# Layer 0 of a four-layer gated cross-attention network: the order of the last row transfers out, and the grain of the adds of the rows that come back

## The chip, the cores and the metric

The kernel runs on one core of a Trainium2 chip. A core has five engines that matter here, each with its own list of instructions that it runs strictly in order: TensorE (PE, matrix products), VectorE (DVE), ScalarE (ACT), GpSimd (POOL) and SyncE (SP), which issues transfers. Transfers run on sixteen DMA engines beside them. The metric is the device time of one execution in microseconds, lower is better; the number given is the median of several executions.

## The reference, cut to what matters

The input x has 16 sequences of 128 tokens and 128 features. Four layers follow one another, each an attention to a context and a feed-forward part, both added to x through a gate:

```python
x = x + tanh(g_xattn[0]) * _L0_xattn_ref(_layernorm(x), ctx)
x = x + tanh(g_ffn[0])   * _L0_ffn_ref(_layernorm(x), Wr, Wg, Wu, Wd)
x = x + tanh(g_xattn[1]) * _L1_xattn_ref(_layernorm(x), ctx, ...)
x = x + tanh(g_ffn[1])   * _L1_ffn_ref(_layernorm(x), ...)
...   # layers 2 and 3: two more attentions, a slot mixture, a second routed feed-forward

# _L0_ffn_ref: 8 experts, each token uses 2 of them
topk_vals, topk_idx = top_k(flat @ Wr, 2);  topk_w = softmax(topk_vals)
combine = sum(one_hot(topk_idx, 8) * topk_w)
out = sum over e of  (silu(flat @ Wg[e]) * (flat @ Wu[e])) @ Wd[e] * combine[:, e]
```

What matters for the change is that the feed-forward part of layer 0 sends each token to two of eight experts, and that its result is added to x before the attention of layer 1 normalizes x. The feed-forward part of layer 1 has 16 routed experts and two shared ones.

## The kernel before, in words

**Groups.** The 16 sequences form four groups of four (512 tokens). X[g] holds a group's x in on-chip memory as 128 partitions x 4 sequences x 128 features. Work on different groups is interleaved: the attention of one group runs while the experts of another fill TensorE.

**Layer 0, feed-forward.** Group 0 is computed densely, all 8 experts (16 half-experts of width 128) for all tokens. Groups 1 to 3 (`BYE` = 1) are computed sparsely: `choose_0` normalizes and routes them, `places_0` counts tokens by expert and gives every (token, choice) a row in a table `xd` in device memory, sorted by expert. Twenty-four indirect transfers on GpSimd (line 941, one for each of 12 sequences and 2 choices) scatter the rows into `xd`. `blocks_0` loads `xd` back in blocks of 128 rows by SP (line 1005), transposes them on TensorE (line 1012), multiplies each with the weights of its one expert (lines 1034 and 989) and writes the result to `yd` (line 997). `return_0` gathers the rows back with 24 indirect transfers on GpSimd (line 1072), and VectorE adds each, times its weight, to X[g] (line 1064).

**Experts.** `experts` is one stream of all dense experts, in the order of `ORDER`. `gated` (lines 445 to 471) does one half-expert n: two matrix products `pg` and `pu` (lines 450, 451), a gating `sg` on ScalarE and VectorE (lines 455 to 458), the product `h` on VectorE (lines 460, 462), and its weighting by the routing `hw`, on GpSimd (line 470), or on VectorE (line 468) for a few experts that `on_vector` names. `hw` is left out for the shared experts, which in layer 1 are n = 0 and 1. The third product `acc` follows `LAG` = 2 experts later (line 1089). The weight of the routing reaches the chip's partitions through a transfer `cb` (line 433). After each expert the stream takes some steps of other work that is listed for that n: routing of the next group, and from three lists the steps of the sparse part. `SEND` says after which experts of group 0 of layer 0 a scatter is issued (15 of 24; the other 9 follow after the last expert, in the loop `for _ in sending`). `FETCH` says after which experts of layer 1 a gather is issued: two each after n = 0 to 3 of group 0, one each after n = 4 to 17, and one each after n = 0 and 1 of group 1. `ADD` says where the adds are written: those of group 1 at n = 6 of group 0, of group 2 at n = 14, of group 3 at n = 4 of the next.

**Main order.** The main program pulls the stream with `until(layer, g)` until that group's result is in X[g], then writes the instructions of the next attention, for example `until(0, 0); attention_1(0); until(0, 1); attention_1(1)`. The stream stops at every `yield what`, so what the attention writes comes between two pieces of it. An attention begins with `normed`: statistics of X[g] on VectorE, `ve` (line 255), the power `rs` on GpSimd (line 257), and the scaling `xn` on VectorE (line 268); `transposed` follows on TensorE (line 241) and `add_row` adds a bias to X[g] on GpSimd (line 279).

**What sets the order.** When the program is built, a planner orders each engine's instructions: it simulates the engines with its own costs, and gives a free engine the ready instruction that was written earliest. An instruction that is written late but ready early can thus be placed ahead of others. The order is fixed on the chip. `behind_of(what, ins)` adds an edge to it: `ins` is placed behind the last instruction recorded in `latest[what]`, on the same engine, without a wait. `latest["h"]` is the last product h, `latest["hw"]` the last hw on GpSimd. Scatters and gathers are ordered behind the hw last written. Of the eight adds of a group only the first (t = 0, k = 0) is ordered behind an h; the second of a sequence follows the first because both write the same part of X[g].

Buffers with one tag share their place. The normalized rows that the scatters read (`xs`, in `choose_0`) have the tag `kTm` with one place, which the keys `kT` of the first attention of layer 1 use next.

Of the kernel before, what the change touches and what calls it, by code (L numbers as in the profile page):

```python
# [14 lines left out]
ALU = mybir.AluOpType  # L15
# [4 lines left out]
GB = 4  # L20
# [14 lines left out]
BYE = 1  # L35
# [24 lines left out]
def flamingo(ctx, tc, x_in, ctx_in, mask_in, w1, w2, w3, wslot, wsmall, slots, cols_in, rows_in, consts_in,  # L60
# [51 lines left out]
    def behind_of(what, ins):  # L112

        if what in latest:
            in_turn([latest[what]], ins)
# [130 lines left out]
    def normed(g, xn=None, on_act=False):  # L246
        x = X[g]
        st = small.tile([P, GB, 6], F32, tag=tag_of("st"), name="st")
        mv = small.tile([P, GB, 2], F32, tag=tag_of("mv"), name="mv")
        for t in range(GB):  # L250
            nc.vector.bn_stats(st[:, t, :], x[:, t, :])  # L251
        for t in range(GB):
            nc.vector.bn_aggr(mv[:, t, :], st[:, t, :])
        ve = small.tile([P, GB], F32, tag=tag_of("ve"), name="ve")
        nc.vector.tensor_scalar(ve[:], mv[:, :, 1], EPS, None, ALU.add)  # L255
        rs = small.tile([P, GB], F32, tag=tag_of("rs"), name="rs")
        nc.gpsimd.tensor_tensor(rs[:], ve[:], neghalf[:], ALU.pow)  # L257
        if xn is None:
            xn = act.tile([P, GB, D], F32, tag=tag_of("xn"), name="xn", bufs=1)
        if on_act:  # L260
            off = small.tile([P, GB], F32, tag="off", name="off")
            nc.gpsimd.tensor_tensor(off[:], mv[:, :, 0], rs[:], ALU.mult)
            nc.gpsimd.tensor_scalar(off[:], off[:], -1.0, None, ALU.mult)
        for t in range(GB):
            if on_act:
                nc.scalar.activation(xn[:, t, :], x[:, t, :], AF.Identity, bias=off[:, t:t + 1], scale=rs[:, t:t + 1])
            else:
                nc.vector.tensor_scalar(xn[:, t, :], x[:, t, :], mv[:, t, 0:1], rs[:, t:t + 1], ALU.subtract, ALU.mult)  # L268
        return xn
# [588 lines left out]


    SEND = [(n, 1 + (n + 1) % 2) for n in range(6, 16)]  # L860
    FETCH = {0: [(n, 2) for n in range(4)] + [(n, 1) for n in range(4, 18)], 1: [(0, 1), (1, 1)]}
    ADD = {0: [(6, 1), (14, 2)], 1: [(4, 3)]}

    def on_vector(layer, g, n):

# [39 lines left out]
    def places_0():  # L905
# [32 lines left out]
        for t in range(NT):  # L938
            for k in range(2):
                yield  # L940
                ins = nc.gpsimd.indirect_dma_start(  # L941
                    out=xd[:], out_offset=bass.IndirectOffsetOnAxis(ap=to[:, k, t:t + 1], axis=0), in_=xs[:, t, :],
                    in_offset=None)
                apart("xd", ins)
                behind_of("hw", ins)

    def owners_0():
        tmp, v, nb, two, comb, to = placed[0]
# [105 lines left out]
    def return_0():  # L1054

        to, by, _ = places[0]
        for g in range(BYE, NG):
            tags = ("ya", "yb") if (g - BYE) % 2 else ("xns", "xnTs")
            ys = [act.tile([P, GB, D], F32, tag=tag, name="y0", bufs=1) for tag in tags]
            t0 = (g - BYE) * GB  # L1060
            def add(g=g, t0=t0, ys=ys):
                for t in range(GB):
                    for k, y in enumerate(ys):
                        ins = nc.vector.scalar_tensor_tensor(X[g][:, t, :], y[:, t, :], by[:, k, t0 + t:t0 + t + 1],
                                                             X[g][:, t, :], ALU.mult, ALU.add)
                        if not t and not k:
                            behind_of("h", ins)
            adds[g] = add

            for t in range(GB):  # L1070
                for k, y in enumerate(ys):
                    ins = nc.gpsimd.indirect_dma_start(
                        out=y[:, t, :], out_offset=None, in_=yd[:],
                        in_offset=bass.IndirectOffsetOnAxis(ap=to[:, k, t0 + t:t0 + t + 1], axis=0))
                    apart(f"y{g}{k}", ins)
                    behind_of("hw", ins)
                    yield

    adds = {}

    def experts():

# [22 lines left out]
        for at, (layer, g) in enumerate(ORDER):  # L1105
# [22 lines left out]
            if layer == 1:  # L1128
                for n, k in FETCH.get(g, ()):
                    steps.setdefault(n, []).extend([("x", fetching, None)] * k)  # L1130
                for n, i in ADD.get(g, ()):
                    steps.setdefault(n, []).append(("x", i, (0, i)))
            acc = []
            for n, (w, k) in enumerate(FW[layer]):
                side[0] = "x"
# [13 lines left out]
                if late and n == LAG:  # L1149
                    late()  # L1150
                for side[0], step, what in steps.get(n, ()):
                    owners_0() if step == "owners" else adds[step]() if isinstance(step, int) else next(step, None)
                    side[0] = "m"
                    if what is not None:
                        yield what
            if moving:
                side[0] = "m"
                for _ in sending:
                    pass
                side[0] = "x"  # L1160
                while behind:
                    down()
                what = end()
                side[0] = "m"
                yield what
                nxt = routing(1, 0)
                for n, _ in enumerate(blocks_0()):
                    if n in (8, 11, 12, 15):
# [243 lines left out]
```

## Time and profile before

| | |
|---|---|
| median of 3 runs | 922.02 us (920.46 to 922.61) |
| profiled execution | 919.22 us, its span 917.5 us |
| granted TensorE clock over the span | 0.972 |
| scatters, line 941 | 24, median 969 ns on GpSimd, landing 2.3 us (median) after issue |
| gathers, line 1072 | 24, median 982 ns on GpSimd, landing 2.4 to 6.7 us after issue, median 3.7 |
| adds of returned rows, line 1064 | 24, median 351 ns, up to 1358 |
| hw on GpSimd, line 470 | 137, mean 1287 ns |

A row of a timeline gives start, length, engine, line, operation, written tile and read tiles, shapes and count, and in brackets how long the engine idled before it and what ended that. A row of waits gives who waited for whom, then the total, the number and the longest wait. A row of the stretch table gives a stretch, its length, the busy time of PE, PE's weight loads, DVE, ACT and POOL with instruction counts, the TensorE clock that was granted as a share of full speed, the busy share of the DMA engines and GB/s. Times count from the span's start. An engine that is not the bottleneck may idle at no cost.

### The profile page before, as it was taken

How to read it: one execution, taken by the hardware profiler on the slowest of the kernel's cores; microseconds unless marked ns; L12 is line 12 of the kernel's file. 1: busy time of each engine (PE TensorE's matmuls, PEld its weight loads, DVE VectorE, ACT ScalarE, POOL GpSimd, SP SyncE). 2: the span in 40 equal slices, each digit the busy share in tenths (PEclk: the TensorE clock that was granted, in tenths of full speed). 3: DMA queues.
4: the chain of work that ended last, by engine and by line, in shares of the span. 5: the costliest groups of instructions: out<-in, count | busy, mean ns of one | idle time of the engine just before them, and what ended most of it. 6: DMA issues, size and time to landing. Idle time of an engine off the chain costs nothing.

```text
span 917.5 us, 16089 instructions
## 1 busy us (share of the span) xinstructions
PE 831.0 (91%) x6191; PEld 464.1 (51%) x6191; DVE 571.5 (62%) x1598; ACT 266.3 (29%) x484; POOL 302.0 (33%) x312
## 2 busy tenths in 40 slices
PE   5897599889879999999999999999989999999997
PEld 4553399335335454455455545555554544454443
DVE  4673244566777647567686777668666668666522
ACT  2522355231313222322223222233212331222321
POOL 5448421456533114112422113231114123313443
PEclk9899699899999999999999999999999999999999
DMA  9351122631211002101202112310102111211231
GB/s 303 125 124 39 54 70 77 214 111 49 70 53 58 25 2 81 36 25 35 73 22 70 40 43 85 101 36 25 36 13 73 48 36 46 83 48 48 95 106 32
DMA packets 55677, 62.12 MB, mean 68 GB/s; under 512 B 14312, under 2 KB 33512, under 8 KB 55472
## 3 DMA queue, kind: packets, MB, share of 16 engines
q1 hardware_dynamic: 53536, 57.67, 20.5%
q0 software_dynamic: 1536, 3.15, 1.1%
q8 instruction: 49, 0.80, 0.4%
q10 hardware_dynamic: 528, 0.26, 0.1%
q14 instruction: 28, 0.23, 0.1%
HBM read 53.97 MB, written 7.09 MB: 67 GB/s over the span
## 4 chain that ended last, share of the span: by engine, by line
PE 48%; DVE 20%; POOL 13%; issue 9%; DMA 5%; ACT 4%; POOLq 0%; SPq 0%; DVEq 0%; ACTq 0%
PE mm L108 8%; POOL hw L470 6%; PE acc L1089 6%; PE pg L450 6%; PE pu L451 5%; DVE mp L490 3%; DVE sg L456 3%; PE mm L617 2%; PE po L496 2%; POOL xd L941 2%; DVE h L462 2%; DMA y<-yd,to 2%; POOL rs L257 2%; PE po L499 2%; PE mm L612 2%
## 5 line engine op out<-in xcount | busy, mean ns | idle before, releaser
L470 POOL TENSOR_TENSOR hw<-h,cb 128x512 f32<-128x512 f32 x137 | 176.2, 1287 | 443.5 <-DVE h L462 353.7
L451 PE MATMUL pu<-xnTx,wall 128*128 128x512 f32 x288 | 154.4, 618 | 10.5 <-DVE sg L456 9.0
L450 PE MATMUL pg<-xnTx,wall 128*128 128x512 f32 x288 | 153.4, 615 | 1.1 <-ACT xnTx L243 0.7
L1089 PE MATMUL acc<-hw,wall 128*128 128x512 f32 x288 | 152.2, 612 | 1.5 <-POOL hw L470 1.5
L455 ACT ACTIVATE sg<-pg 128x512 f32<-128x512 f32 x123 | 73.4, 598 | 240.2 <-PE pg L450 236.4
L462 DVE TENSOR_TENSOR h<-sg,pu 128x512 f32<-128x512 f32 x145 | 99.0, 683 | 54.8 <-PE pu L451 35.6
L456 DVE SCALAR_TENSOR_TENSOR sg<-sg,pg 128x512 f32<-128x512 f32 x123 | 83.5, 679 | 48.7 <-ACT sg L455 48.4
L451 PEld LDWEIGHTS pu<-xnTx,wall 128*128 128x128 f32 x288 | 51.9, 194 | 72.5 <-issue 39.8
L1089 PEld LDWEIGHTS acc<-hw,wall 128*128 128x128 f32 x288 | 54.4, 196 | 60.8 <-issue 52.4
L490 DVE TENSOR_REDUCE mp<-mm 128x4 f32<-128x512 f32 (+1 forms) x112 | 65.8, 644 | 21.1 <-PE mm L617 19.9
L450 PEld LDWEIGHTS pg<-xnTx,wall 128*128 128x128 f32 x288 | 49.7, 192 | 42.4 <-issue 29.8
L504 DVE RECIPROCAL rcw<-po 128x128 f32<-128x128 f32 (+1 forms) x28 | 25.2, 899 | 53.6 <-PE po L499 42.6
L639 ACT ACTIVATE pts<-mm 128x512 f32<-128x512 f32 x64 | 33.8, 602 | 77.1 <-PE mm L633 77.0
L496 PE MATMUL po<-pts,vp 128*32 128x128 f32 (+1 forms) x896 | 46.0, 273 | 7.0 <-ACT pts L639 6.5
L257 POOL TENSOR_TENSOR rs<-ve,neghalf 128x4 f32<-128x4 f32 x32 | 32.9, 1027 | 58.8 <-DVE ve L255 55.0
L268 DVE TENSOR_SCALAR xn<-x,mv,rs 128x128 f32<-128x128 f32 x96 | 33.1, 402 | 24.1 <-POOL rs L257 24.1
L499 PE MATMUL po<-pts,own 128*32 128x128 f32 (+1 forms) x896 | 44.1, 265 | 0.6 <-issue 0.6
L241 PE MATMUL tr<-ident,xn 128*128 128x128 f32 x100 | 22.4, 310 | 19.2 <-DVE xn L268 17.0
L496 PEld LDWEIGHTS po<-pts,vp 128*32 128x32 f32 (+1 forms) x896 | 21.4, 108 | 30.3 <-ACT pts L639 14.8
L251 DVE BATCH_NORM_STATS2 st<-x 128x6 f32<-128x128 f32 x128 | 29.3, 280 | 7.4 <-DMA x<-in_x 6.8
L458 ACT ACTIVATE sg<-pg 128x512 f32<-128x512 f32 x33 | 19.5, 595 | 48.8 <-PE pg L450 48.6
L241 PEld LDWEIGHTS tr<-ident,xn 128*128 128x128 f32 x100 | 12.6, 142 | 35.9 <-issue 14.6
(346 smaller groups left out, 1249.4 us busy)
## 6 DMA issues: line engine op xcount, KB each, us to landing
cb<-combD SPq DMA_DIRECT2D x72, 256.0 KB, 3.3
cb<-combD SPq DMA_DIRECT2D x128, 128.0 KB, 2.9
wall<-in_gu SPq DMA_DIRECT2D x24, 256.0 KB, 4.4
wall<-in_dn SPq DMA_DIRECT2D x12, 256.0 KB, 4.3
xb<-xd SPq DMA_DIRECT2D x7, 256.0 KB, 2.8
yd<-yb SPq DMA_DIRECT2D x7, 256.0 KB, 2.5
xd<-vp SPq DMA_DIRECT2D x1, 1072.0 KB, 7.6
x<-in_x SPq DMA_DIRECT2D x4, 256.0 KB, 4.7
```

The lines of the kernel that those rows point to most:

```text
L108: nc.tensor.matmul(out=o, lhsT=l, rhs=r, start=start, stop=stop)
L257: nc.gpsimd.tensor_tensor(rs[:], ve[:], neghalf[:], ALU.pow)
L450: in_turn(chain, nc.tensor.matmul(out=pg[:], lhsT=w[:, 0], rhs=xnT[:], start=True, stop=True))
L451: in_turn(chain, nc.tensor.matmul(out=pu[:], lhsT=w[:, 1], rhs=xnT[:], start=True, stop=True))
L455: nc.scalar.activation(sg[:], pg[:], AF.Tanh, scale=0.5)
L456: nc.vector.scalar_tensor_tensor(sg[:], sg[:], 1.0, pg[:], ALU.add, ALU.mult)
L462: ins = nc.vector.tensor_tensor(h[:], sg[:], pu[:], ALU.mult)
L470: latest["hw"] = nc.gpsimd.tensor_tensor(hw[:], h[:], cb[:], ALU.mult).ins
L490: nc.vector.tensor_reduce(mp[:, 0:n, 32 * i + 16:32 * i + 18], src, AX.X, ALU.max)
L496: in_turn(chain, nc.tensor.matmul(out=po[32 * jj:32 * jj + 32, 0, :], lhsT=vcols, rhs=pts, start=first, stop=last, skip_group_check=True))
L499: in_turn(chain, nc.tensor.matmul(out=po[32 * jj:32 * jj + 32, 1, :], lhsT=own[rows, r, :], rhs=pts, start=False, stop=last, skip_group_ch ...
L1089: in_turn(chain, nc.tensor.matmul(out=acc[0][:], lhsT=w[:, 2], rhs=h[:], start=n == 0, stop=last))
```

## The change

The scatters: after the last expert of group 0 of layer 0 four instead of nine are written at once. The other five are written after the stream has yielded, which is after the first attention of layer 1 has been written, and are ordered behind `latest["rs"]`, the power of that attention's norm, instead of behind an hw. `normed` records that power.

The adds: instead of eight at a time from `ADD`, each is written on its own. `return_0` keeps a list of gathers written; once it holds more than four, each further gather's step also writes the oldest one's add, ordered behind the h last written. Four more steps write the last four. `FETCH` for group 1 of layer 1 is one step after each of n = 0 to 5, of which the first two write a gather and an add and the other four an add alone. When the last add of a group is written the stream reports the group as done, which is at n = 7 and n = 15 of group 0 and n = 5 of group 1, instead of n = 6, 14 and 4. Numbers of gathers, scatters and adds stay.

```diff
--- before.py
+++ after.py
@@ -254,7 +254,7 @@
         ve = small.tile([P, GB], F32, tag=tag_of("ve"), name="ve")
         nc.vector.tensor_scalar(ve[:], mv[:, :, 1], EPS, None, ALU.add)
         rs = small.tile([P, GB], F32, tag=tag_of("rs"), name="rs")
-        nc.gpsimd.tensor_tensor(rs[:], ve[:], neghalf[:], ALU.pow)
+        latest["rs"] = nc.gpsimd.tensor_tensor(rs[:], ve[:], neghalf[:], ALU.pow).ins
         if xn is None:
             xn = act.tile([P, GB, D], F32, tag=tag_of("xn"), name="xn", bufs=1)
         if on_act:
@@ -858,8 +858,7 @@
 
 
     SEND = [(n, 1 + (n + 1) % 2) for n in range(6, 16)]
-    FETCH = {0: [(n, 2) for n in range(4)] + [(n, 1) for n in range(4, 18)], 1: [(0, 1), (1, 1)]}
-    ADD = {0: [(6, 1), (14, 2)], 1: [(4, 3)]}
+    FETCH = {0: [(n, 2) for n in range(4)] + [(n, 1) for n in range(4, 18)], 1: [(n, 1) for n in range(6)]}
 
     def on_vector(layer, g, n):
 
@@ -942,7 +941,9 @@
                     out=xd[:], out_offset=bass.IndirectOffsetOnAxis(ap=to[:, k, t:t + 1], axis=0), in_=xs[:, t, :],
                     in_offset=None)
                 apart("xd", ins)
-                behind_of("hw", ins)
+                behind_of(sent_behind[0], ins)
+
+    sent_behind = ["hw"]
 
     def owners_0():
         tmp, v, nb, two, comb, to = placed[0]
@@ -1054,29 +1055,31 @@
     def return_0():
 
         to, by, _ = places[0]
+        landed = []
+
+        def add():
+
+            g, t, k, y = landed.pop(0)
+            i = (g - BYE) * GB + t
+            behind_of("h", nc.vector.scalar_tensor_tensor(X[g][:, t, :], y, by[:, k, i:i + 1], X[g][:, t, :], ALU.mult,
+                                                          ALU.add))
+            return g if (t, k) == (GB - 1, 1) else None
+
         for g in range(BYE, NG):
             tags = ("ya", "yb") if (g - BYE) % 2 else ("xns", "xnTs")
             ys = [act.tile([P, GB, D], F32, tag=tag, name="y0", bufs=1) for tag in tags]
-            t0 = (g - BYE) * GB
-            def add(g=g, t0=t0, ys=ys):
-                for t in range(GB):
-                    for k, y in enumerate(ys):
-                        ins = nc.vector.scalar_tensor_tensor(X[g][:, t, :], y[:, t, :], by[:, k, t0 + t:t0 + t + 1],
-                                                             X[g][:, t, :], ALU.mult, ALU.add)
-                        if not t and not k:
-                            behind_of("h", ins)
-            adds[g] = add
-
             for t in range(GB):
                 for k, y in enumerate(ys):
+                    i = (g - BYE) * GB + t
                     ins = nc.gpsimd.indirect_dma_start(
                         out=y[:, t, :], out_offset=None, in_=yd[:],
-                        in_offset=bass.IndirectOffsetOnAxis(ap=to[:, k, t0 + t:t0 + t + 1], axis=0))
+                        in_offset=bass.IndirectOffsetOnAxis(ap=to[:, k, i:i + 1], axis=0))
                     apart(f"y{g}{k}", ins)
                     behind_of("hw", ins)
-                    yield
-
-    adds = {}
+                    landed.append((g, t, k, y[:, t, :]))
+                    yield add() if len(landed) > 4 else None
+        while landed:
+            yield add()
 
     def experts():
 
@@ -1128,8 +1131,6 @@
             if layer == 1:
                 for n, k in FETCH.get(g, ()):
                     steps.setdefault(n, []).extend([("x", fetching, None)] * k)
-                for n, i in ADD.get(g, ()):
-                    steps.setdefault(n, []).append(("x", i, (0, i)))
             acc = []
             for n, (w, k) in enumerate(FW[layer]):
                 side[0] = "x"
@@ -1149,20 +1150,25 @@
                 if late and n == LAG:
                     late()
                 for side[0], step, what in steps.get(n, ()):
-                    owners_0() if step == "owners" else adds[step]() if isinstance(step, int) else next(step, None)
+                    done = owners_0() if step == "owners" else next(step, None)
+                    if step is fetching and done:
+                        what = (0, done)
                     side[0] = "m"
                     if what is not None:
                         yield what
             if moving:
                 side[0] = "m"
-                for _ in sending:
-                    pass
+                for _ in range(4):
+                    next(sending)
                 side[0] = "x"
                 while behind:
                     down()
                 what = end()
                 side[0] = "m"
                 yield what
+                sent_behind[0] = "rs"
+                for _ in sending:
+                    pass
                 nxt = routing(1, 0)
                 for n, _ in enumerate(blocks_0()):
                     if n in (8, 11, 12, 15):
```

## The prediction, made before the changed kernel was run

> **What bounds the kernel now.** I read the page's busy shares first, then the chain of work that ended last, then idle time by engine in each stretch, then the timelines of GpSimd (POOL), VectorE (DVE) and TensorE (PE) around the two edits.
>
> ```profile
> span 917.5 us, 16089 instructions
> PE 831.0 (91%) x6191; PEld 464.1 (51%) x6191; DVE 571.5 (62%) x1598; ACT 266.3 (29%) x484; POOL 302.0 (33%) x312
> ```
>
> TensorE is the bound overall, so time can only come out of stretches where it idles or runs at a reduced clock. The stretch table gives it 1.73 us busy of 14 between 87 and 101 us, 105.1 of 124 between 161 and 285, and 146.8 of 155 between 285 and 440. The edits touch the first two.
>
> First hole, in the order DVE, POOL, PE (start, length, operation, and in brackets the idle time before it):
>
> ```profile
> 91.42 0.21 DVE L255 TENSOR_SCALAR ve<-mv 128x4 f32<-128x4 f32 x1
> ...
> 98.32 0.97 POOL L941 DMA_INDIRECT xd<-xs,to  x1 [0.31 <-issue]
> 99.31 1.06 POOL L257 TENSOR_TENSOR rs<-ve,neghalf 128x4 f32<-128x4 f32 x1
> ...
> 101.17 1.15 PE L241 MATMUL tr<-ident,xn 128*128 128x128 f32 x4 [11.77 <-DVE xn L268]
> ```
>
> The norm's input `ve` is there at 91.63, but its power `rs` starts at 99.31: ten scatters stand ahead of it from 86.82 on, and TensorE idles 11.77 us.
>
> The second stretch, waits between 161 and 285 us (total, times, longest):
>
> ```profile
> DVE x L1064 <- DMA y<-yd,to: 19.8, 10, 3.3
> ...
> PE pu L451 <- DVE sg L456: 7.0, 2, 3.8
> ...
> PE mm L108 <- DVE aT L578: 4.7, 1, 4.7
> ```
>
> VectorE stood 19.8 us ahead of the adds of returned rows, each with its gather still in flight. Behind it TensorE stopped three times: 3.81 us until 174.84, 3.16 until 204.53 and 4.74 until 255.45, and each stop is followed by a stretch at about half clock (column after POOL: PEclk):
>
> ```profile
> 174.50:181.50 7.00, 6.66 (x9) 2.79 (x10) 5.32 (x16) 0.60 (x1) 3.94 (x4) 0.54 0.60 166
> 204.50:208.50 4.00, 3.97 (x9) 1.87 (x10) 2.63 (x5) 0.00 (x0) 2.96 (x3) 0.57 0.06 24
> 255.40:260.10 4.70, 4.65 (x13) 2.79 (x14) 3.62 (x14) 0.64 (x2) 0.78 (x1) 0.64 0.01 2
> ```
>
> Time lost to the clock is length x (1 - clock): 7.0 x 0.46 = 3.2, 4.0 x 0.43 = 1.7, 4.7 x 0.36 = 1.7 us. So the three stops cost 7.0, 4.9 and 6.4 us.
>
> **Why the adds run early.** They are written at experts 6 and 14 of group 0 and expert 4 of group 1, but only the first of each eight is ordered behind an `h`. The other six (t = 1, 2, 3) have no order, and the planner put them where it believed their rows had landed: one group's stand at 173.8 to 178.6, before expert 6.
>
> **Part 1, five scatters move behind `rs`.** A scatter takes 0.97 us and 0.30 to the next, 1.27. Five fewer ahead of `rs` bring it from 99.31 to 99.31 - 6.35 = 92.96, still after `ve` (91.63), so the whole shift counts for the norm. The five left then follow: rs 1.06, scatters 6.35, and probably the bias add L279 (1.27), written earlier and ready once `xn` is done. Last scatter: starts about 100.8 instead of 98.32, lands 2.3 later at 103.1. Who waits: the row loads xb on SP's queue (issued at 100.61 before, landing at least 2.8 us later), so rows are there at 105.9; and the keys kT of this attention, whose buffer is the one the scatters read from (108.33 - 6.35 = 102.0 wanted, 103.1 possible, 1.1 us). TensorE transposed the first rows at 110.06, because attention held it until then; now attention's scores end near 104.8 and the rows come at 105.9. Gain 110.06 - 105.9 = **4.2 us**. Bounds: 6.35 if the scatters' tail is hidden; -2.5 if the planner puts the first row transposes ahead of attention, so that all of it waits for the later scatter. I take 4.2, the value that both timelines give. The clock brings nothing: the hole is still near 5.4 us, longer than all three stops above that ended cold. 101.8 to 105.9 holds attention, so no second hole but 1 us.
>
> **Part 2, each add alone, behind its own `h`, four gathers later.** The 24 adds stay (0.35 us), as do the 24 gathers, their order behind `hw` and their queue; removed is the freedom to run early. Add i now stands behind h of expert i from i = 4 on; gather i behind hw of expert i - 4. An expert takes six matmul halves, 3 x 0.86 = 2.57 us, so four are 10.3 us at least; gathers 8 to 23 landed 3.3 to 5.5 us after issue. So none of these is waited for.
> - Stop 2 (add at 200.22, gather issued 195.50): gone, 4.9 us.
> - Stop 3 (adds at 250.10, 252.53, 254.45, which held the attention's aT at 254.72 while its input was there at 249): they now follow h of experts 3, 4, 5 of group 1. Gone, 6.4 us.
> - Stop 1 stays. Gathers 0 to 7 go out in one burst from 166.18, before any hw on GpSimd, and add 0 and 1 are written at expert 2, whose h ends at 168.0. Gathers 0 and 1 land at 172.9 and 173.5. The planner believed gather 2 landed before the gating of expert 3, so it will believe that of 0 and 1, and VectorE stands until 173.5 as it did until 173.8. Gain 0 (bounds -0.5 to 7.0).
>
> Here the row and the skill part. The Trainium skill, DMA: Bandwidth & Descriptors, section Anatomy of one DMA, gives a GpSimd-issued transfer 2.0 us plus bytes at 436 GB/s: 64 KB would be 2.15 us (estimate), gather 0 would land at 168.3, and stop 1 would vanish too, for 7.0 more. The row says 6.7 us, in a stretch with the DMA engines 93% busy with cb and weight loads. I take the row.
>
> **What the later add costs.** Attention 1, 2 and 3 start one expert later. The three norms behind the last adds (rs at 187.99, 231.08, 270.24) made TensorE wait 1.05, 1.71 and 1.79 us. Where experts fill TensorE, an expert's delay is nothing; without them it costs 2.57 each time. The cover is thinnest at the last, so I charge half an expert, **1.3 us**, with 0 and 7.7 as bounds. Next late would be group 1's routing: its cb loads were issued from 246.73, landed about 4 us later, and its first hw on GpSimd started at 262.30; of 11.6 us slack stop 3 takes 6.4 and one expert 2.6, leaving 2.6.
>
> A rule speaks against this part. The skill, GPSIMD Engine Reference, section Key points, says that GpSimd shares its SBUF interfaces with VectorE, to the cost of VectorE instructions with two SBUF inputs, and the add is one. The trace agrees: 3 of 24 adds took 1.24 to 1.36 us, each while an hw multiply ran:
>
> ```profile
> 184.73 0.69 DVE L462 TENSOR_TENSOR h<-sg,pu 128x512 f32<-128x512 f32 x1
> 185.34 1.62 DVE L1064 SCALAR_TENSOR_TENSOR x<-y,by,x 128x128 f32<-128x128 f32 x2
> ...
> 185.50 1.31 POOL L470 TENSOR_TENSOR hw<-h,cb 128x512 f32<-128x512 f32 x1 [0.56 <-DVE h L462]
> ```
>
> Twenty adds now stand near an hw. By the rule each would cost 0.9 more, 18 us of VectorE. But the three adds that stood directly behind an h took 0.344 to 0.346: they start before hw does, and it is their second that was caught. One add for each h is thus the safe one; I take 0.
>
> **Sum.** 4.2 + 4.9 + 6.4 - 1.3 = 14.2 us. The profiled execution took 919.22 (span 917.5 and 1.7 around it): 905.0, span 903.3. The median shown is 922.02, 2.8 higher, and is what the time is measured by: 922.0 - 14.2 = **907.8**. As a check from the other side: if 161 to 285 idled at the rate of 285 to 440 (5.3%) plus stop 1, idle would fall from 18.9 to 10.4, and with 3.4 of clock that is 11.9, against the 10.0 in my sum. Past 285 I change nothing, but the planner lays that part out anew; I allow 3 us either way.
>
> **Rivals.**
> - *Stop 1 goes too* (the first adds land behind the gating of expert 3): for it, add 1 needs only a small move in the plan; against it, the planner's belief above. 907.8 - 7.0 = 900.8.
> - *The gain turns into a new wait*: experts run ahead, attentions start late, and the routing's 2.6 us of slack is overdrawn, or the planner's new layout uncovers VectorE (84.2 busy of 124). Only half of part 2 and of part 1 would stay: 922.0 - 7 = 915.
> - *It doesn't do what it says*: the bottleneck around 87 to 101 merely moves to the scatters' landing (gain 0 there) and the planner's adds still precede their rows. About 921.
> - *Slower*: the shared port. If the hw multiply catches the adds behind h from expert 4 on, 20 x 0.9 = 18 us go onto VectorE. Between experts alone it has about 1.2 us free in 2.57 and swallows them; inside attention it doesn't. It decides once more than 14.2 / 0.9 = 16 of 20 are both caught and on the path; with all, 907.8 + 18 = 925.8. Against it: the three rows of 0.344.
>
> **How the numbers follow.** Forecast 0.60, stop 1 gone too 0.10, gain half lost 0.14, no change 0.05, slower 0.11. A measurement can tell about 0.2% (1.8 us) from no change. Faster: 0.60 + 0.10 + 0.14 = 0.84; same 0.05; slower 0.11. The range 900 to 919 leaves out slower, no change and a little below; the forecast's own is 903 to 913.
>
> **What would show it.** `rs` of the first attention starts 6 us earlier relative to the last hw of layer 0, with five scatters behind it; TensorE's hole there falls from 11.8 to 5 to 6 us; rows are transposed about 4 us earlier. The adds' wait falls from 19.8 us to about 4, all before 174 in the old count; the holes before 204.5 and 255.4 and their cold stretches are gone; adds stay at 0.35 us. It is wrong if adds at experts 8 and on still wait for gathers, if they take 1.2 us, if TensorE waits for cb at the start of group 1, or if rows and keys wait for the scatters longer than 2 us.

## The result, and the profile after

The changed kernel takes **907.33 us** (median of 6 runs, 905.23 to 910.81), the kernel before 922.02 (920.46 to 922.61, 6 runs beside them). The ratio is 0.9844, with a 95% interval of 0.9826 to 0.9863: 14.7 us less, where 14.2 were forecast.

The profiled execution of the changed kernel took 908.96 us, 1.6 above its median; that of the kernel before, 919.22, lies 2.8 below. So the two profiles are only 10.3 us apart. The page of the changed kernel, span and busy shares:

```profile
span 907.3 us, 16095 instructions
PE 832.2 (92%) x6191; PEld 465.8 (51%) x6191; DVE 571.6 (63%) x1597; ACT 267.6 (29%) x485; POOL 302.0 (33%) x312
```

TensorE does the same work (832.2 us against 831.0); only its idle time has shrunk. The stretch table of the changed kernel says where:

```profile
87.00:101.00 14.00, 5.68 (x14) 2.28 (x13) 3.36 (x14) 1.17 (x2) 11.77 (x13) 0.78 0.12 37
161.00:285.00 124.00, 112.50 (x367) 55.84 (x366) 91.08 (x259) 34.92 (x58) 66.67 (x65) 0.96 0.33 102
285.00:440.00 155.00, 145.78 (x1243) 76.55 (x1243) 103.18 (x251) 40.11 (x70) 37.07 (x35) 1.00 0.12 38
```

TensorE is busy 5.68 us instead of 1.73 in the first stretch, 112.5 instead of 105.1 in the second, and about as long as before in the third (145.8 against 146.8).

**The first hole.** The timeline of the changed kernel, GpSimd and TensorE, in order of time:

```profile
94.07 0.97 POOL L940 DMA_INDIRECT xd<-xs,to  x1 [0.31 <-issue]
95.05 0.62 POOL L1029 COPY wb<-wall 128x512 f32 x1
95.63 1.05 POOL L257 TENSOR_TENSOR rs<-ve,neghalf 128x4 f32<-128x4 f32 x1
...
97.20 1.33 PE L241 MATMUL tr<-ident,xn 128*128 128x128 f32 x4 [5.92 <-DVE xn L268]
...
103.28 0.96 POOL L940 DMA_INDIRECT xd<-xs,to  x1 [0.30 <-issue]
...
108.50 0.66 PE L1013 MATMUL tr<-ident,xb 128*128 128x128 f32 x4 [0.74 <-DMA xb<-xd]
```

The last scatter ahead of `rs` starts at 94.07; five follow it, the last at 103.28. TensorE idles 5.92 us ahead of the normed rows instead of 11.77. The first rows of the table are transposed at 108.50 after a wait of 0.74 us, for their transfer and not for attention. What counts is the distance to the end of layer 0's first group, the transposes of yT: they stand at 88.51 before and at 90.62 now (the two executions differ by 2.1 us already there, ahead of the edit). From there to the first rows it was 21.55 us and is 17.88.

**The second stretch.** The waits of the changed kernel between 155 and 275 us:

```profile
PE tr L241 <- DVE xn L268: 5.6, 5, 1.9
DVE x L1064 <- DMA y<-yd,to: 4.8, 1, 4.8
PE pu L451 <- DVE sg L456: 4.3, 3, 3.6
```

VectorE waits for a returned row once, for 4.8 us, instead of ten times for 19.8. The wait of attention for `aT` (4.7 us) is gone. The timeline of the changed kernel shows what is left:

```profile
164.67 1.08 POOL L1074 DMA_INDIRECT y<-yd,to  x1 [7.95 <-DMA yd<-yb]
...
171.31 0.35 DVE L1064 SCALAR_TENSOR_TENSOR x<-y,by,x 128x128 f32<-128x128 f32 x1 [4.76 <-DMA y<-yd,to]
...
173.18 1.91 PE L451 MATMUL pu<-xnTx,wall 128*128 128x512 f32 x2 [3.63 <-DVE sg L456]
...
189.07 1.10 PE L241 MATMUL tr<-ident,xn 128*128 128x128 f32 x4 [1.91 <-DVE xn L268]
...
203.18 1.65 POOL L470 TENSOR_TENSOR hw<-h,cb 128x512 f32<-128x512 f32 x1 [0.32 <-DVE h L462]
203.62 1.36 DVE L1064 SCALAR_TENSOR_TENSOR x<-y,by,x 128x128 f32<-128x128 f32 x1
```

The stop near 174 us stays (3.63 us): gather 0 is issued at 164.67 and its add starts at 171.31, 6.6 us later. The stops that ended at 204.53 and 255.45 are gone. Of the 24 adds 22 take 0.32 to 0.42 us; two take 1.36 and 1.59. Fifteen of the 24 stand directly behind an `h`, and the two long ones are not among them. The one shown, of 1.36 us, stands elsewhere and starts inside an hw multiply.

**A table by stage.** The transposes of yT that end each group's experts are a mark that every version has. The column on the left runs from the one of layer 0's group 0 to the one of layer 1's group 0, the next from there to group 1's, both in the profiled executions. Work can move across the mark between the two, so their sum is the safer figure. All later stages together differ by 4.6 us between two executions of one and the same kernel (after, and after again), so the table stops there.

| kernel | median, us | first stage | second stage | both |
|---|---|---|---|---|
| before | 922.0 | 172.2 | 99.8 | 272.0 |
| after | 907.33 | 157.5 | 101.5 | 258.9 |
| after again, another chip | 909.32 | 158.4 | 101.4 | 259.8 |
| scatters only | 918.82 | 169.2 | 99.8 | 269.0 |
| adds only | 911.11 | 161.9 | 101.4 | 263.3 |
| order only | 917.63 | 162.1 | 104.6 | 266.7 |
| order, hw on VectorE | 913.97 | 158.7 | 106.7 | 265.3 |
| lag of one | 917.29 | 165.2 | 101.9 | 267.1 |
| lag of two | 908.02 | 158.9 | 101.2 | 260.2 |
| lag of eight | 917.66 | 158.5 | 111.0 | 269.5 |
| all nine scatters | 911.83 | 162.8 | 101.4 | 264.3 |
| first adds held | 905.26 | 155.8 | 101.5 | 257.3 |
| held, hw on VectorE | 900.67 | 150.4 | 101.4 | 251.9 |
| held, norms too | 901.43 | 151.2 | 99.9 | 251.1 |

The change gains 14.7 us in the first stage and gives 1.7 back in the second. Nearly all of the gain is idle time of TensorE. The first stage in the stretch table, before, then after:

```profile
88.51:260.70 172.19, 141.39 (x721) 93.49 (x722) 91.66 (x276) 58.51 (x103) 71.13 (x78) 0.91 0.29 89
90.62:248.09 157.47, 140.07 (x713) 93.35 (x714) 88.29 (x262) 58.59 (x103) 70.08 (x77) 0.93 0.31 95
```

TensorE idles 30.8 us before and 17.4 after. But it works as long at half clock, 17.6 us before and 17.5 after (18.6 in the other execution of the changed kernel), which loses half of that, 8.8 and 8.7 us. The cold stretches behind the stops at 204.53 and 255.45 are gone, and two others have come, behind waits for normed rows of 1.91 us near 189 and 1.64 near 219. Behind the first hole the cold stretch now holds more work, 7.2 us instead of 4.6.

### The profile page after: what moved, and what is told of

The parts are those of the page before. It is cut to its first block, busy times and chain, and to the rows that moved or that the text cites. A ratio compares the mean times of both kernels' runs of the same rounds, so it can differ in the third digit from the quotient of the medians.

```text
span 907.3 us, 16095 instructions
## 1 busy us (share of the span) xinstructions
PE 832.2 (92%) x6191; PEld 465.8 (51%) x6191; DVE 571.6 (63%) x1597; ACT 267.6 (29%) x485; POOL 302.0 (33%) x312
## 5 line engine op out<-in xcount | busy, mean ns | idle before, releaser
L455 ACT ACTIVATE sg<-pg 128x512 f32<-128x512 f32 x123 | 73.5, 598 | 264.1 <-PE pg L450 251.1
L1092 PE MATMUL acc<-hw,wall 128*128 128x512 f32 x288 | 149.9, 604 | 1.5 <-POOL hw L470 1.5
L268 DVE TENSOR_SCALAR xn<-x,mv,rs 128x128 f32<-128x128 f32 x96 | 35.5, 426 | 21.5 <-POOL rs L257 21.2
L241 PE MATMUL tr<-ident,xn 128*128 128x128 f32 x100 | 22.9, 310 | 13.4 <-DVE xn L268 12.2
L617 PE MATMUL mm<-kTm,qT 32*128 32x256 f32 x256 | 30.6, 414 | 0.0
```

The lines of the kernel that those rows point to most:

```text
L455: nc.scalar.activation(sg[:], pg[:], AF.Tanh, scale=0.5)
L617: nc.tensor.matmul(out=split(ps[i])[:, 2 * s:2 * s + 2, :], lhsT=qT[rr, s, b], rhs=kTm[rr, s, :, b], start=False, stop=True, skip_group_ch ...
L1092: in_turn(chain, nc.tensor.matmul(out=acc[0][:], lhsT=w[:, 2], rhs=h[:], start=n == 0, stop=last))
```

## The experiments

The kernel before was run beside each group of experiments and had a median of 922.08 to 922.18 us there. Where a ratio is given it is to those runs.

**Scatters only.** The first part of the change, put into the kernel before:

```diff
+                behind_of(sent_behind[0], ins)      # "hw", and "rs" for the last five
-                for _ in sending:
-                    pass
+                for _ in range(4):
+                    next(sending)
                 ...
                 yield what
+                sent_behind[0] = "rs"
+                for _ in sending:
+                    pass
```

> Only the five scatters move behind rs; the adds stay as in the kernel before. If the two parts add up, this is worth the 4 us of part 1: about 918, with the hole before the first attention at about 6 us instead of 11.8 and the rows transposed about 21 us after the last hw of layer 0 begins (24.7 before). If the moved scatters only push the wait to the rows' landing, 921 to 922. If it only pays together with the adds, 922.

918.82 us, ratio 0.9962 (0.9948 to 0.9975): 3.3 us less. Timeline of this kernel, TensorE:

```profile
96.53 1.33 PE L241 MATMUL tr<-ident,xn 128*128 128x128 f32 x4 [5.60 <-DVE xn L268]
...
107.83 0.66 PE L1014 MATMUL tr<-ident,xb 128*128 128x128 f32 x4 [0.98 <-DMA xb<-xd]
```

The hole is 5.60 us, and the rows come 17.87 us after the transposes of yT (at 89.96), as in the full change: 3.7 us earlier than before. Halving the hole by some 6 us is thus worth 3.7 at the rows, since the scatters that give up their place are late for them.

**Adds only.** The changed kernel with all nine scatters where they were:

```diff
-                for _ in range(4):
-                    next(sending)
+                for _ in sending:
+                    pass
```

> Only the adds change (each alone, behind its own h, four gathers later); the scatters stay as before. Theory: the stops before 204.5 and 255.4 us go, worth 11.3 less about 1.3: about 911 to 912, and the waits for returned rows fall from 19.8 us to about 4 to 5, all at the first adds. Rival, that the gain is all from the scatters: 921.

911.11 us, ratio 0.989 (0.9859 to 0.992): 11.0 us less. With the 3.3 of the scatters that makes 14.3, against 14.7 for both: the parts add up. Over the two stages they save 3.0 and 8.6, against 13.1 for both (12.2 in the other execution of the changed kernel).

**All nine scatters behind `rs`.** Does a scatter that is late hold up rows and keys, as the first part's working has it?

```diff
-                for _ in range(4):
+                for _ in range(0):
                     next(sending)
```

> The changed kernel with all nine remaining scatters behind rs instead of five. rs is then limited by its input (about 91.6 against 93 in the profile before), so the norm gains 1 to 2 us at most, while the last scatter still stands behind rs and the bias add. Theory: rows and keys wait for the last scatter, which comes no earlier; the time is 907, the same as the changed kernel within 1.5 us. If the norm is what sets the time, 904 to 905.

911.83 us, ratio 0.9881 (0.9851 to 0.9911), 4.5 more than the changed kernel: the expectation was wrong. Timeline of this kernel:

```profile
93.27 1.05 POOL L257 TENSOR_TENSOR rs<-ve,neghalf 128x4 f32<-128x4 f32 x1 [2.98 <-DVE ve L255]
...
105.99 0.95 POOL L940 DMA_INDIRECT xd<-xs,to  x1 [0.30 <-issue]
...
108.31 0.69 ACT L286 ACTIVATE kTm<-mm,cols 128x512 f32<-128x512 f32 x1 [5.73 <-DMA xd<-xs,to]
...
109.06 2.07 PE L108 MATMUL mm<-kTm,qT 128*128 128x128 f32 x8 [5.45 <-ACT kTm L286]
```

`rs` now waits for `ve`, so GpSimd stands idle for 2.98 us that scatters could have used. The keys wait 5.73 us for the last scatter, because they go into the buffer that it reads from; TensorE idles 5.45 us behind them and its next products are slow. The shared buffer that the first part named is real. With five scatters moved it is not felt; with nine it decides.

**Order only.** The kernel before, its three batches of eight adds where they were, but each add ordered behind an h:

```diff
-                        if not t and not k:
-                            behind_of("h", ins)
+                        behind_of("h", ins)
```

> The kernel before, with one edit: each of a group's eight adds, not only the first, is ordered behind the h last written; they stay in batches of eight at the old places, no lag is added. If what costs is the freedom to run ahead of the rows, this alone takes all waits away, the first stop too (7.0 + 4.9 + 6.4 us, less some 2 for VectorE being held by eight adds at a time): about 906. If the gain needs the fine grain (single adds spread over the experts), it stays near 920 or is slower than 922.

917.63 us, ratio 0.9946 (0.9925 to 0.9966): 4.5 us less, between the two expectations. No add waits for a row, and the stop near 174 is gone. But each batch now holds VectorE in one piece. Timeline of this kernel:

```profile
180.02 5.15 DVE L1064 SCALAR_TENSOR_TENSOR x<-y,by,x 128x128 f32<-128x128 f32 x8
...
186.86 2.08 PE L451 MATMUL pu<-xnTx,wall 128*128 128x512 f32 x2 [3.21 <-DVE sg L456]
...
240.88 1.02 PE L421 MATMUL tr<-ident,comb 128*16 128x128 f32 x4 [2.14 <-DVE comb L378]
...
266.11 1.10 PE L241 MATMUL tr<-ident,xn 128*128 128x128 f32 x4 [3.04 <-DVE xn L268]
```

Eight adds at 0.35 us would be 2.8; the first batch takes 5.15, with two hw multiplies of GpSimd in that time. The gating behind it is late, and TensorE idles 3.21 us. The other two batches take 3.27 and 3.20 us and push the routing and the norm. In the first stage the order alone saves as much as the adds alone, 10.1 us and 10.3, since the stop near 174 goes with it; it gives 4.8 back in the second, where they give 1.6.

**Order only, with the hw of those experts on VectorE.** How much of that is GpSimd's multiply, how much the batch itself?

```diff
-        ... or (layer, g) == (1, 0) and n < 4
+        ... or (layer, g) == (1, 0) and (n < 4 or n in (6, 7, 14)) or (layer, g) == (1, 1) and n == 4
```

> The kernel before with all eight adds of a batch ordered behind their h (as in the run that did the order alone), and hw of the experts of these batches (6, 7 and 14 of group 0, 4 of group 1) on VectorE. If the shared port is a share of what that run fell short by, a batch of eight takes about 2.8 us rather than 5.15, 3.27 and 3.20, and the time is 913 to 915. If the batch's own length is all of it (eight adds in one piece hold VectorE past the next gating), 917 to 918.

913.97 us, ratio 0.9916 (0.9889 to 0.9944), 3.7 less than with hw on GpSimd and within the time of the first reading. Timeline of this kernel, VectorE, then TensorE:

```profile
180.72 1.65 DVE L1064 SCALAR_TENSOR_TENSOR x<-y,by,x 128x128 f32<-128x128 f32 x1
182.30 0.68 DVE L468 TENSOR_TENSOR hw<-h,cb 128x512 f32<-128x512 f32 x1
182.90 1.65 DVE L1064 SCALAR_TENSOR_TENSOR x<-y,by,x 128x128 f32<-128x128 f32 x6
184.68 0.33 DVE L1064 SCALAR_TENSOR_TENSOR x<-y,by,x 128x128 f32<-128x128 f32 x1
...
186.50 1.13 PE L451 MATMUL pu<-xnTx,wall 128*128 128x512 f32 x2 [2.10 <-DVE sg L456]
```

Eight adds now take 1.65 + 1.65 + 0.33 = 3.63 us in the first batch (one is still caught by an earlier expert's hw on GpSimd) and 2.34 in the others, although VectorE has four more multiplies. So multiplies on GpSimd do stretch a batch. What that costs in time stays open: the intervals of the two runs overlap, and their two stages together differ by 1.4 us, not 3.7. Some 3 us remain to the adds taken one by one (911.11). They go with the grain, since eight at once stand in front of a gating, and with the later places of the adds; no run changed one of these without the other.

**Lag of one, two and eight gathers instead of four.**

```diff
-                    yield add() if len(landed) > 4 else None
+                    yield add() if len(landed) > 1 else None       # 1, 2 or 8
```

(and as many steps of group 1 in `FETCH` as the last adds need)

> The changed kernel with a lag of one gather. One expert is 2.57 us, the row needs about 5 to 6.5 us after its h: each of some 16 adds waits 2 to 3.5 us with VectorE stopped behind it. Expected: waits for rows 25 to 45 us, time 920 to 935. If the lag plays no role and only the order behind h does, 907.

> The changed kernel with a lag of two gathers instead of four. A gather leaves about 1.4 us after its h ends and lands 3.3 to 5.5 us later; two experts are 5.1 us at TensorE's pace. So from expert 6 on an add waits 0 to 1.5 us and hardly stops TensorE; the norms come two experts earlier; the first adds are written at expert 1 and wait as before. Expected 905 to 911. If four is needed to cover the transfers, 915 or more.

> The changed kernel with a lag of eight gathers: the first add is written at expert 4, so no add waits and the first stop goes (7 us), while each attention of groups 1 to 3 starts four experts later. If an expert's delay is hidden by the experts that fill TensorE: about 901 to 903. If the later norms cost what I charged (half an expert for one expert of delay, so 5 us for four more): 905 to 907, with TensorE idle before the norms and before the cb of group 1.

A lag of one: 917.29 us, ratio 0.9929 (0.9902 to 0.9957), better than the 920 to 935 expected. The waits of VectorE and TensorE in this kernel between 155 and 275 us:

```profile
DVE x L1064 <- DMA y<-yd,to: 12.4, 9, 5.3
...
PE tr L421 <- DVE comb L378: 4.0, 1, 4.0
```

Nine adds wait for their rows again, though for 12.4 us and not the 25 to 45 expected. A lag of two: 908.02 us, ratio 0.9866 (0.9809 to 0.9923), as expected: one wait for a row, 5.4 us, the first. Two experts, about 5 us, are thus enough for a gather, and one (2.57 us) is not.

A lag of eight: 917.66 us, ratio 0.9962 (0.9947 to 0.9977), where 901 to 907 were expected, because the stop near 174 goes. It does go, and the first stage is no shorter for it; the second is 9.5 us longer than after the change. Timeline of this kernel, TensorE:

```profile
195.78 1.24 PE L241 MATMUL tr<-ident,xn 128*128 128x128 f32 x4 [3.17 <-DVE xn L268]
...
222.75 0.47 PE L241 MATMUL tr<-ident,xn 128*128 128x128 f32 x1 [2.76 <-DVE xn L268]
...
239.10 1.02 PE L421 MATMUL tr<-ident,comb 128*16 128x128 f32 x4 [4.91 <-DVE comb L378]
```

The attentions start four experts later still, and TensorE waits for norms and then for the next group's routing. Over both stages it idles 31.3 us instead of 23.3 and loses 11.3 us to the half clock instead of 8.7, which makes the 10.5 by which they are longer. (The second stage is longer because work has moved into it: 104.2 us busy instead of 95.5.) That the experts which would cover these waits have been used up is the likely reason; no run tests it.

**First adds held.** The change's own lag, but the first eight adds, whose gathers go out in one burst, wait until experts 4, 5 and 6 (three, three, two). This asks what the stop near 174 is worth. It moves something else too: the last of the eight is written at expert 6 instead of 7, so the norm behind them comes an expert earlier.

```diff
+    HOLD = {n: 0 for n in range(8)}
+    HOLD.update({8: 3, 9: 3, 10: 2, 11: 0})
...
-                    yield add() if len(landed) > 4 else None
+                    done = None
+                    for _ in range(HOLD.get(i + i + k, 1)):
+                        done = add() or done
+                    yield done
```

> The changed kernel with one more edit: the first eight adds are held until experts 4, 5 and 6 of group 0 (three, three, two), the rest stays. Theory: the stop that stayed (3.6 us idle and the half clock behind it) is the wait of adds 0 and 1, written two experts after a burst of gathers that takes 5 to 7 us to land; held, it goes, and the time is about 901. Rival: the stop moves to the next thing that is late, the cb transfers of these experts, and the time is that of the changed kernel, 907.

905.26 us, ratio 0.9806 (0.977 to 0.9841): 2.1 us better than the change, where 6 were expected, and not clear of noise, since the two intervals overlap. The stop is gone, TensorE is busy 15.87 of the 16 us from 160 on, and new ones follow. Timeline of this kernel:

```profile
176.92 1.99 DVE L1067 SCALAR_TENSOR_TENSOR x<-y,by,x 128x128 f32<-128x128 f32 x1
...
177.46 1.28 POOL L470 TENSOR_TENSOR hw<-h,cb 128x512 f32<-128x512 f32 x1
...
179.87 1.13 PE L451 MATMUL pu<-xnTx,wall 128*128 128x512 f32 x2 [1.53 <-DVE sg L456]
...
184.46 1.25 POOL L470 TENSOR_TENSOR hw<-h,cb 128x512 f32<-128x512 f32 x1
184.50 2.06 DVE L268 TENSOR_SCALAR xn<-x,mv,rs 128x128 f32<-128x128 f32 x4 [0.42 <-POOL rs L257]
...
185.85 0.59 PE L241 MATMUL tr<-ident,xn 128*128 128x128 f32 x2 [3.13 <-DVE xn L268]
```

An add beside an hw takes 1.99 us instead of 0.35. The last of the eight ends later than it would alone, the norm with it, and TensorE idles 1.53 and 3.13 us.

**Held, with hw on VectorE.** The same, and hw of experts 4 to 6 on VectorE, so that no multiply of GpSimd runs beside the held adds; the changed kernel unchanged ran on the same chip beside it.

```diff
-        ... or (layer, g) == (1, 0) and n < 4
+        ... or (layer, g) == (1, 0) and n < 7
```

> The kernel after with the first eight adds held to experts 4, 5 and 6 (as in the run that held them), and with the gating multiply hw of experts 4, 5 and 6 of group 0 moved from GpSimd to VectorE, so that no GpSimd multiply runs beside the held adds. Theory, that GpSimd's multiply on a shared port stretched the held adds and made the new stops: the adds take 0.35 us each, the TensorE stop of 1.5 us near 180 us is gone, and the time is 902 to 903. Rival, that three adds for one h are too many for VectorE whatever GpSimd does: the stop stays (VectorE also gets three multiplies of about 0.7 us) and the time is 905 or more.

> The kernel after, unchanged, on the same chip as the two runs that hold the first adds: 907 us within 1.5, so that these can be compared with it directly.

**900.67 us** (900.31 to 900.93), ratio 0.9765 (0.9731 to 0.9798). The changed kernel beside it took 909.32 (906.31 to 912.55), ratio 0.9848 (0.9808 to 0.9887), 2 us more than the first time and just outside its expectation, with the same ratio to before. That is 8.6 us, and the executions of the two do not overlap: this version beats both kernels. Timeline of this kernel:

```profile
181.53 1.12 PE L451 MATMUL pu<-xnTx,wall 128*128 128x512 f32 x2 [1.95 <-DVE sg L456]
181.64 1.05 POOL L257 TENSOR_TENSOR rs<-ve,neghalf 128x4 f32<-128x4 f32 x1 [3.64 <-DVE ve L255]
...
186.09 1.79 DVE L1067 SCALAR_TENSOR_TENSOR x<-y,by,x 128x128 f32<-128x128 f32 x1
```

All eight held adds, at 171.78 to 179.68, take 0.30 to 0.35 us each; the add at 186.09 is the next one. It stands directly behind its `h` and is caught all the same: GpSimd is then at the bias add of line 279 (185.23 to 186.51) and goes on to an hw. The time is better than expected, but not by the stop that was named: the stop for the gating stays (1.95 us, as the rival has it, since VectorE now also has three multiplies). What went is the stop for the normed rows, 3.13 us with the hold alone: `rs` starts at 181.64 instead of 183.42, with GpSimd waiting for `ve`, and TensorE does not idle for it at all. From 176 to 200 us TensorE is busy 22.05 us of 24 instead of 19.07. Against the changed kernel, which has 22.09 there, the gain lies at the stop: TensorE is busy all 16 us from 160 on instead of 12.37. The first stage is 7.0 us shorter, 3.3 of it idle time and 3.3 clock (10.9 us of work at half clock instead of 17.5).

**Held, and hw on VectorE ahead of the next norms too.**

```diff
-        ... or (layer, g) == (1, 0) and n < 7
+        ... or (layer, g) == (1, 0) and (n < 7 or n == 15) or (layer, g) == (1, 1) and n == 5
```

> The same with hw on VectorE also for the two experts ahead of the next norms (expert 15 of group 0, expert 5 of group 1), so that the norm's power rs does not queue behind a multiply on GpSimd. Theory, that the waits for the normed rows (1.9 and 1.6 us in the kernel after, each followed by a slow clock) come from that queue: they shrink to under 1 us and the time is 900 to 902. Rival, that the waits come from the last add itself being late: they stay, and the time is that of the run before, within 1 us.

901.43 us (900.16 to 904.58), ratio 0.9777 (0.9737 to 0.9818): no different from the version before it. TensorE's waits for normed rows: the last falls from 1.41 us to 0.22, the one of 1.64 stays. That one could not fall: it belongs to the norm of the next group's routing, which follows no group's last add, and GpSimd idles 5.0 us ahead of its `rs`, waiting for `ve`. The wait behind the last add of group 2, where expert 15 was moved, is 0.83 us instead of 1.03. Both numbers expected fit this time, so it doesn't tell the readings apart; in the traces the queue on GpSimd made the last wait and little of the other. The second stage is 1.6 us shorter and the first 0.8 longer.

## Why the prediction was right, point by point

**Part 1, `rs` earlier.** Forecast 6.35 us, measured 5.8: from the last hw of layer 0 to `rs` it was 13.9 us and is 8.15. The missing 0.6 is the copy of `wb` (0.62 us) that the planner put ahead of `rs`. Last scatter forecast 2.5 later, measured 2.9. Rows forecast 4.2 us earlier, measured 3.7; the time, 3.3 in the run with this part alone. The clock was forecast to bring nothing: in that run TensorE idles 4.5 us less in the first stage and loses 9.9 us to the half clock instead of 8.8. Whether the edit costs that 1.1 is open: with the adds alone, where this hole is as before, its cold stretch loses 1.2 more too. The gate that was named, the scatters' landing, is what the first transpose of rows waits for now, and the other one, the keys' buffer, appears where all nine scatters are moved.

**Part 2, stops.** That stop 1 stays and stops 2 and 3 go was right; 4.9 + 6.4 - 1.3 = 10.0 was forecast for this part, and the run with it alone gained 11.0. The row taken for the landing of gather 0, 6.7 us against the 2.15 estimated from the Trainium skill (DMA: Bandwidth & Descriptors, Anatomy of one DMA), measured 6.6: with 2.15 the stop would have gone. (Over that flight in the kernel before, 166.18 to 172.90, the DMA engines were 87% busy, a little less than the 93% read.)

**The clock, where it was wrong.** Of the 11.3 us for stops 2 and 3, 3.4 were the cold stretches behind them, and these were not gained. With the adds alone TensorE idles 8.2 us less in the first stage, close to the 7.9 forecast for idle time (3.2 and 4.7), but still loses 8.3 us to the half clock instead of 8.8: a wait of 1.64 us for normed rows (1.0 in the kernel before) is followed by 6.8 us at half clock (222.16 to 228.98 in that run), and the cold stretch at the first hole, which that run leaves as it was, loses 1.2 us more. The forecast took a stop and its cold stretch to leave together, and put the clock behind new waits at nothing.

**Luck in the sum.** 14.2 against 14.7 is closer than its terms. Part 1 came out 0.9 us lower than forecast and part 2 1.0 higher, each within the noise of its run. Over the two stages that the edits touch, the profiled executions save 13.1 us, and the adds alone 8.6 where 10.0 were forecast; the rest of the medians' difference lies outside them, where two executions of one kernel differ by 4.6 us in the later stages alone.

**The later add.** 1.3 us were charged for attentions that start an expert later; the second stage is 1.7 us longer in the changed kernel and 1.6 with the adds alone. In the first the charge is not seen apart from the rest. The lag of eight shows that this is a price that runs away: four experts more cost 10.5 us over both stages.

**The shared port.** Taken at nothing, with all the weight on an add directly behind its h: all 15 adds that stand there agree, with 0.34 to 0.42 us, so the slower rival falls for this change. Of the nine elsewhere two were caught. The place is not safe in itself: in the kernel with held adds and hw on VectorE an add directly behind its `h` took 1.79 us (at 186.09), while GpSimd was still at an earlier instruction. Such adds lose up to 1.6 us each, where that rival took 0.9; the order-only kernel with hw on VectorE was 3.7 us faster by the medians and 1.4 over the two stages. It may also be a share of the difference between 905.26 and 900.67; there the moved multiplies cleared GpSimd's queue ahead of `rs` too, and the two weren't tried apart.

**Where the account was incomplete.** "Why the adds run early" names the missing order as the cause, and nothing else. The order alone gives 4.5 us of the 11.0 (5.3 of 8.6 over the two stages). The rest comes with the grain and the later places: one add for each h, where eight in one piece hold VectorE past a gating and meet several multiplies. The sum didn't suffer, since it was built from the stops that vanish, not from the cause.

**The rivals.** *Stop 1 goes too* was priced at 7.0 us more; removing the stop gave 2.1 (against the changed kernel's first measurement, and not clear of noise), and 8.6 with three multiplies moved off GpSimd, where the first stage shrinks by the 7.0. In both the norm also comes an expert earlier. What these multiplies bring without the hold wasn't tried. *The gain turns into a new wait* described the lag of eight, 917.66, in mechanism and nearly in size (915). The check by idle time forecast 10.4 us of idle between 161 and 285; it is 11.5.

## What to carry to other kernels

Work that may run early must be ordered behind something that runs late, and in pieces small enough for the gaps of its engine: here the order gave 4.5 us, and single adds at later places 6.5 more. When a transfer or an add is pushed back, price the next waiter on both sides: five scatters moved gained 3.3 us and nine lost 4.5 against the five, a lag of two to four gathers was the best, one and eight were both some 10 us worse. Before a stop on one engine is removed, look at what will then run beside what: removing the one near 174 brought 2.1 us, within the noise, and 8.6 together with three multiplies moved off GpSimd. Price the clock behind the waits that come as well as behind those that go: here 13.4 us of idle time went and none of the clock's loss.

## What the runs showed of the hardware

The TensorE clock does not follow the length of an idle stretch alone. The wait for normed rows of 1.9 us near 189 us occurs in two executions of the changed kernel. The stretch table of the first, four us behind that wait, then behind a later one:

```profile
190.00:194.00 4.00, 4.00 (x7) 1.52 (x7) 2.03 (x4) 1.87 (x3) 3.49 (x3) 0.57 0.06 20
221.00:225.00 4.00, 3.82 (x5) 1.70 (x6) 1.94 (x6) 0.72 (x2) 2.28 (x2) 0.57 0.05 16
```

The same table of the other execution (after again):

```profile
190.00:194.00 4.00, 4.00 (x10) 1.46 (x9) 1.60 (x3) 2.85 (x5) 2.98 (x3) 1.00 0.16 46
219.00:223.00 4.00, 3.97 (x5) 1.85 (x6) 1.81 (x6) 0.60 (x1) 2.28 (x2) 0.50 0.10 27
```

The clock (third column from the end) is 0.57 behind the first wait in one execution and 1.00 in the other. The second wait, 1.64 us and 0.68 shortly behind it, is followed by half clock in both, and by full clock in the version with held adds and hw on VectorE, whose waits there are as long. A slow stretch of 4 us costs 4 x 0.43 = 1.7 us, so waits under 2 us can cost about twice their length, or nothing more.

The traces show what decides it. In the clock records of all 14 the grant changes only at a fixed step: from one change to the next it is 3.41 us or a multiple of that. Cut at these steps, the wait of 1.9 us lies within one step in the first execution and across two in the other. The stretch table of the first:

```profile
187.04:190.46 3.42, 1.51 (x7) 0.78 (x6) 1.72 (x5) 0.25 (x1) 2.17 (x3) 1.00 0.50 156
```

And of the other:

```profile
184.22:187.63 3.41, 2.40 (x6) 0.76 (x4) 1.60 (x5) 0.60 (x1) 3.08 (x4) 1.00 0.89 321
187.63:191.04 3.41, 2.50 (x8) 1.27 (x9) 2.66 (x7) 1.09 (x2) 2.07 (x3) 1.00 0.26 68
```

TensorE is busy 44% of the one step, and half clock follows; 70% and 73% of the two, and it doesn't. Over all 14 traces half clock followed each of the 49 steps at full clock in which TensorE was busy under 40% of the time, none of the 3231 with 75% or more, and 54 of the 211 between. Where the steps' borders fall differs between executions of one kernel, so the price of a wait under 2 us is in part chance.

An add of 0.35 us beside a GpSimd multiply took up to 1.99 us. The scaling of four normed rows took 2.06 us where an hw starts right behind `rs`, in the changed kernel too (at 218.06), and 1.12 where none does (at 188.67). Of the 171 adds that stand directly behind an `h` in the 14 traces, 14 took over 0.5 us, twelve of them while GpSimd was at an instruction begun earlier. In the record of the first kernel with held adds the add at 176.92 even starts before the multiply (177.46), and ends behind it.
